# Softmax rows turned by DMA through DRAM, in 16-bit halves, instead of on TensorE: two attention and two expert layers on one core

## The chip, the cores and the metric

The kernel runs on one core of one Trainium2 chip. The metric is the device time of one execution in microseconds; lower is better. The kernel before takes 2253.72 us, the median of 3 runs (2252.45 to 2257.0).

## What is computed

Eight sequences of 512 tokens, 256 features wide, in float32, go through four layers, each added to its input:

```python
x = x + attn_a(layernorm(x))      # 16 heads of 64, a distance penalty per head
x = x + experts(layernorm(x))     # RMS norm, best 2 of 8 experts, gated MLP
x = x + attn_b(layernorm(x))      # 8 heads of 128, rotary embedding
x = x + experts(layernorm(x))

# both attentions, per head
s = q @ k.T                       # plus penalty, or scaled; causal mask
p = softmax(s, axis=-1)           # [512 queries, 512 keys]
out = (p @ v) @ w_out
```

Only the causal half of `s` is computed: for each tile of 128 queries, numbered `it`, the keys up to its own tile. That makes 4 row blocks of 128, 256, 384 and 512 columns, 1280 columns in all, ten 128x128 squares per head.

## The kernel before, in words

**Order of the work.** `layer` (L1133) walks through 64 steps, one for each sequence `b` (8) and group `g` (8). A group is 128 feature columns: two heads in attention a, one in attention b. `Attention.step` (L503) writes out TensorE's order by hand (L120 keeps it so); the tile framework orders the other engines and the queues, and puts in the waits. A step has: the scores of the current group (`scores`, L356, in three banks); the transposes of the group before (`turn`, L436); the projection of queries and keys of the next group (`project`, L327); pieces of other work (`extra`), such as values, output projection, norms, the expert layer's routing; and last the average of the group before (`average`, L461). So a group's scores open one step and its average closes the next.

**One group.** `scores` multiplies queries with keys into PSUM; DVE adds the penalty or mask and takes the row minimum of the negated scores (L407); ACT takes the exponential and the row sum (L417). After the third bank DVE inverts the sums (L428), and the rows are divided in place in the tile `S` (L434): the 512-column block on DVE, the other three on POOL. `turn` then transposes the ten squares of a head on TensorE into PSUM (L449), in three banks, and ACT (L459), for one bank of the second head DVE (L457), copies them to `PT`. `average` takes `PT` as the moving operand, with the values as weights (L476), four matmuls per head of 512, 384, 256 and 128 columns.

**Buffers.** `S` has four buffers, `PT` two, `qk` (queries and keys of a group in one tile) two, `tmp` three. PSUM has eight banks, all under one tag.

**Expert layers.** `Experts` sorts tokens by expert during the attention layer (`sorting`, L917) and then runs 71 blocks of 128 rows (`run`, L1049): POOL gathers rows (L939), TensorE transposes and multiplies, POOL scatters. `flush` (L1192) says at which block the pieces left over from attention are run, the last transposes (L1185) and the last average among them.

**SP's queue** issues the loads, the stores of normed rows (`h_all`, L619) and of the residual (`x_mid`, L621), and the loads of expert results (L1078), in order.

Of the kernel before, what the change touches and what calls it, by code (L numbers as in the profile page):

```python
# [36 lines left out]
F32 = mybir.dt.float32  # L38
BF16 = mybir.dt.bfloat16
I32 = mybir.dt.int32  # L40
AF = mybir.ActivationFunctionType
ALU = mybir.AluOpType
# [19 lines left out]
S_OFF = {3: 0, 2: 512, 0: 896, 1: 1024}  # L62
S_BANKS = [(3,), (2, 0), (1,)]

P_OFF = {0: 0, 1: 512, 3: 896, 2: 1024}
P_BANKS = [(0,), (1, 3), (2,)]
PACKED = 1280
# [18 lines left out]
AHEAD = 3  # L86
# [7 lines left out]
def layers(  # L94
# [109 lines left out]
    step_p = iota([P, TOTAL], [[P, TOTAL]], "step_p")  # L204
    spare = iota([P, TOTAL], [[P, TOTAL]], "spare", 1, 4 * PLANE)
    tiles = iota([P, 2, NB * NT], [[32, 2], [1, NB * NT]], "tiles", 0, 64)
    before = const.tile([P, P], F32, tag="before", name="before")
    nc.vector.tensor_scalar(before, lane, part, None, ALU.is_gt)
    ones = const.tile([P, P], F32, tag="ones", name="ones")
    nc.vector.memset(ones, 1.0)  # L210

# [68 lines left out]
    class Attention:  # L280
# [46 lines left out]
        def project(self, b, g, j):  # L327
# [3 lines left out]
            if j == 0:  # L331
                self.qk[b, g] = work.tile([P, 2, T], F32, tag="qk", name=f"qk_{key}")
            qk = self.qk[b, g]
# [10 lines left out]
            if kind == "b":  # L344
                h = DB // 2
                rot = work.tile([P, T], F32, tag="tmp", bufs=3, name=f"rot_{key}_{j}")
                nc.vector.tensor_tensor(rot[0:h], pp[h:P], sin_sb[h:P], ALU.mult)
                nc.vector.tensor_tensor(rot[h:P], pp[0:h], sin_sb[0:h], ALU.mult)
                nc.vector.tensor_tensor(qk[:, j, :], pp, cos_sb, ALU.mult)  # L349
                nc.gpsimd.tensor_tensor(qk[:, j, :], qk[:, j, :], rot, ALU.add)  # L350
            elif j == 0:
                nc.scalar.mul(qk[:, 0, :], pp, DA**-0.5)
            else:
                nc.vector.tensor_copy(qk[:, 1, :], pp)  # L354

        def scores(self, b, g, n):  # L356
# [3 lines left out]
            qk = self.qk[b, g]  # L360
            if n == 0:
                rows = []
                for i in range(nh):
                    rows.append(
                        (
                            work.tile([P, PACKED], F32, tag="S", bufs=4, name=f"S_{key}_{i}"),
# [5 lines left out]
                if kind == "a":  # L372
                    add = []
                    for i in range(nh):
                        a = work.tile([P, T], F32, tag="tmp", bufs=3, name=f"ali_{key}_{i}")
# [14 lines left out]
            at = {it: S_OFF[it] - S_OFF[bank[0]] for it in bank}  # L390
            for it in bank:
                w = (it + 1) * P
                for i in range(nh):
# [3 lines left out]
                        lhsT=qk[r, 0, it * P : (it + 1) * P],  # L397
                        rhs=qk[r, 1, 0:w],
# [3 lines left out]
            for i, (S, nm, sums) in enumerate(self.S[b, g]):  # L402
                for it in bank:
                    w = (it + 1) * P
                    s = S[:, S_OFF[it] : S_OFF[it] + w]
# [19 lines left out]
            if n == len(S_BANKS) - 1:  # L425
                del self.qk[b, g], self.add[b, g]
                for S, nm, sums in self.S[b, g]:
                    nc.vector.reciprocal(sums, sums)  # L428
                    for it in (3, 2, 0, 1):
                        s = S[:, S_OFF[it] : S_OFF[it] + (it + 1) * P]  # L430

                        mine = it == 3 or (b, g) == (NB - 1, NQ - 1)
                        eng = nc.vector if mine else nc.gpsimd
                        eng.tensor_scalar(s, s, sums[:, it : it + 1], 1.0, ALU.mult, ALU.mult)  # L434

        def turn(self, b, g, i, n):  # L436

            key = f"{self.kind}_{b}_{g}_{i}"
            S = self.S[b, g][i][0]
            if n == 0:  # L440
                self.PT[b, g, i] = work.tile([P, PACKED], F32, tag="PT", name=f"PT_{key}")
            bank = P_BANKS[n]
            base = P_OFF[bank[0]]
            tp = ps.tile([P, T], F32, tag="ps", bufs=8, name=f"tp_{key}_{n}")
            width = 0
            for jt in bank:
                for it in range(jt, NT):
                    o = P_OFF[jt] - base + (it - jt) * P
                    nc.tensor.transpose(  # L449
                        tp[:, o : o + P],  # L450
                        S[:, S_OFF[it] + jt * P : S_OFF[it] + (jt + 1) * P],
                        ident,
                    )
                    width += P
            pt = self.PT[b, g, i][:, base : base + width]
            if n == 0 and i == 1:
                nc.vector.tensor_copy(pt, tp[:, 0:width])  # L457
            else:
                nc.scalar.copy(pt, tp[:, 0:width])  # L459

        def average(self, b, g):  # L461
            kind, nh = self.kind, self.nh
            key = f"{kind}_{b}_{g}"
            del self.S[b, g]
# [8 lines left out]
            for jt in range(NT):  # L473
                for i in range(nh):
                    c0 = (g % 2) * P + i * cols
                    nc.tensor.matmul(  # L476
                        op[i * cols : (i + 1) * cols, jt * P : T],
                        lhsT=v[:, jt, c0 : c0 + cols],
                        rhs=PT[i][:, P_OFF[jt] : P_OFF[jt] + T - jt * P],
                        start=(jt == 0),  # L480
                        stop=(jt == NT - 1),
# [21 lines left out]
        def step(self, last, cur, after, extra):  # L503
# [3 lines left out]
            def scores(n):  # L507
                if cur:
                    self.scores(*cur, n)

            def turn(i, *banks):
                if last:
                    for n in banks:
                        self.turn(*last, i, n)

            def project(j):
                if after and after not in there:
                    self.project(*after, j)

            if self.kind == "a":  # L520
# [818 lines left out]
```

## Time and profile before

| | before |
|---|---|
| median of 3 runs | 2253.72 us |
| the profiled execution | 2251.17 us |
| its span | 2249.4 us |
| attention a, about | 16 to 936 us |
| experts, first layer | 936 to 1177 us |
| attention b | 1177 to 1995 us |
| experts, second layer | 1995 to 2249 us |
| granted TensorE clock, mean | 0.994 |
| HBM read, written | 67.02 MB, 39.60 MB |

All times below are microseconds from the start of the span. In lines of the order of time the columns are start, length, engine, source line, operation, the tile written and the tiles read, and how many instructions were merged; in brackets stands how long the engine had been idle and what released it. Lines of the chain that ended last have start, length, engine, tile, line and count. A float32 matmul appears as two instructions, one for each pass. SPq is SP's queue of DMA issues: the length there is that of issuing, not of the transfer.

### The profile page before, as it was taken

What the parts mean: (1) busy time and instruction counts of PE and PEld (TensorE: products, weight loads), DVE (VectorE), ACT (ScalarE), POOL (GpSimd) and SP (SyncE); (2) the same over time, 40 slices, a digit from 0 to 9 for tenths busy, and PEclk for the clock granted to TensorE, in tenths of its full rate; (3) what the DMA queues carried; (4) which work ended last, traced back from release to release, by engine and by line L of the source; (5) the groups of instructions that cost most, each with busy time, mean ns of one, the idle gap of its engine ahead of it and who ended that gap; (6) DMA issues with size and microseconds to landing.
All of it is one profiled execution on the core that took longest, in us unless ns stands there. A gap on an engine that the chain in (4) does not pass through costs nothing.

```text
span 2249.4 us, 33585 instructions
## 1 busy us (share of the span) xinstructions
PE 2191.5 (97%) x10513; PEld 1430.1 (64%) x10513; DVE 1585.7 (70%) x4817; ACT 961.6 (43%) x2784; POOL 967.7 (43%) x1337
## 2 busy tenths in 40 slices
PE   8999999999999999999999999999999999999995
PEld 5666666666666666656656666666666666666663
DVE  4566666666666687687687676777767678868768
ACT  4555555555555545323334334334433433332331
POOL 5443434343424343366654344333434343346662
PEclk9999999999999999999999999999999999999998
DMA  7100000000000000232220010110101000042237
GB/s 247 38 20 10 18 12 8 22 4 26 1 29 1 29 6 29 103 107 84 86 81 21 10 38 15 34 33 15 47 6 43 8 31 1 19 139 78 85 97 254
DMA packets 78382, 108.80 MB, mean 48 GB/s; under 512 B 9568, under 2 KB 64000, under 8 KB 78208
## 3 DMA queue, kind: packets, MB, share of 16 engines
q1 hardware_dynamic: 62656, 67.58, 9.2%
q0 software_dynamic: 13632, 37.24, 5.2%
q8 instruction: 87, 1.43, 0.3%
q10 hardware_dynamic: 1920, 1.84, 0.2%
q14 instruction: 87, 0.71, 0.1%
HBM read 67.02 MB, written 39.60 MB: 47 GB/s over the span
## 4 chain that ended last, share of the span: by engine, by line
PE 88%; DVE 7%; DMA 1%; issue 1%; ACT 1%; POOL 1%; SPq 0%; DVEq 0%; another core or an unknown queue 0%; ACTq 0%
PE hp_f L982 10%; PE pp_b L337 9%; PE pp_a L337 9%; PE op_a L476 6%; PE sp_a L395 6%; PE tp_a L449 6%; PE sp_b L395 6%; PE op_b L476 5%; PE yp_a L494 5%; PE yp_b L494 5%; PE y_f L1021 5%; PE vp_a L318 4%; PE vp_b L318 4%; PE tp_b L449 3%; PE gtp_f L953 1%
## 5 line engine op out<-in xcount | busy, mean ns | idle before, releaser
L417 ACT ACTIVATE S_a<-S_a,nm_a 128x512 f32<-128x512 f32 (+3 forms) x512 | 280.1, 548 | 311.4 <-DVE nm_a L407 311.2
L350 POOL TENSOR_TENSOR qk_b<-qk_b,rot_b 128x512 f32<-128x512 f32 x128 | 163.1, 1274 | 457.0 <-DVE qk_b L349 434.0
L376 POOL TENSOR_SCALAR ali_a<-alibi 128x512 f32<-128x512 f32 x128 | 79.4, 620 | 454.3 <-DVE nm_a L407 442.0
L982 PE MATMUL hp_f<-we,hT_f 128*128 x544 | 257.8, 596 | 7.6 <-issue 3.9
L417 ACT ACTIVATE S_b<-S_b,nm_b 128x512 f32<-128x512 f32 (+3 forms) x256 | 142.8, 558 | 236.6 <-DVE nm_b L407 228.6
L407 DVE CUSTOM_DVE_ANT_0 S_a<-sp_a,ali_a 128x512 f32<-128x512 f32 (+3 forms) x512 | 215.9, 487 | 30.7 <-PE sp_a L395 28.5
L434 POOL TENSOR_SCALAR S_a<-S_a,sum_a 128x384 f32<-128x384 f32 x378 | 203.1, 554 | 34.6 <-DVE sum_a L428 24.3
L1033 POOL DMA_INDIRECT y_f<-y_f,row_f x142 | 143.5, 1010 | 117.5 <-DVE y_f L1032 58.6
L407 DVE CUSTOM_DVE_ANT_0 S_b<-sp_b,mask 128x512 f32<-128x512 f32 (+3 forms) x256 | 119.3, 484 | 89.1 <-PE sp_b L395 88.9
L395 PE MATMUL sp_b<-qk_b 128*128 128x512 f32 (+3 forms) x512 | 170.5, 436 | 5.5 <-POOL qk_b L350 5.5
L939 POOL DMA_INDIRECT g_f<-h_all_f,token_f x142 | 144.1, 1015 | 61.9 <-issue 39.6
L449 PE MATMUL tp_a<-ident,S_a 128*128 128x128 f32 x1280 | 166.0, 276 | 4.0 <-DVE O_a L484 3.3
L994 ACT ACTIVATE u_f<-u_f 128x256 f32<-128x256 f32 x142 | 59.2, 417 | 256.2 <-DVE u_f L993 176.5
L449 PEld LDWEIGHTS tp_a<-ident,S_a 128*128 128x128 f32 x1280 | 141.3, 142 | 35.1 <-issue 21.6
L476 PE MATMUL op_a<-PT_a,V_a 128*64 128x384 f32 (+3 forms) x1024 | 156.3, 442 | 4.8 <-DVE PT_a L457 2.6
L1021 PEld LDWEIGHTS y_f<-we,aT_f 128*128 128x128 f32 x568 | 108.3, 192 | 77.4 <-issue 58.2
L395 PE MATMUL sp_a<-qk_a 64*128 64x512 f32 (+3 forms) x1024 | 155.5, 443 | 0.9 <-DVE qk_a L354 0.9
L459 ACT COPY PT_a<-tp_a 128x512 f32<-128x512 f32 (+1 forms) x320 | 139.1, 496 | 29.1 <-PE tp_a L449 27.3
L1021 PE MATMUL y_f<-we,aT_f 128*128 x568 | 147.4, 383 | 4.0 <-ACT aT_f L1012 4.0
L476 PE MATMUL op_b<-PT_b,V_b 128*128 128x512 f32 (+3 forms) x512 | 148.6, 433 | 0.0
L993 DVE TENSOR_TENSOR u_f<-hp_f,be 128x512 f32<-128x512 f32 x142 | 98.1, 691 | 65.3 <-PE hp_f L982 27.5
L982 PEld LDWEIGHTS hp_f<-we,hT_f 128*128 128x128 f32 x544 | 92.7, 190 | 76.5 <-issue 70.5
(205 smaller groups left out, 4455.2 us busy)
## 6 DMA issues: line engine op xcount, KB each, us to landing
h_all_f<-hn_f SPq DMA_DIRECT2D x64, 128.0 KB
xm_f<-x_mid_f SPq DMA_DIRECT2D x16, 512.0 KB
yg_f<-y_f SPq DMA_DIRECT2D x32, 256.0 KB
yg_f<-y_f SPq DMA_DIRECT2D x56, 128.0 KB
we<-w_dram SPq DMA_DIRECT2D x8, 512.0 KB
x_mid_f<-x SPq DMA_DIRECT2D x8, 512.0 KB
x_mid_f<-xm_f SPq DMA_DIRECT2D x8, 512.0 KB
x<-x_in_dram SPq DMA_DIRECT2D x7, 512.0 KB
```

The costliest lines, as they stand in the source:

```text
L318: nc.tensor.matmul(vp[:, k, :], lhsT=self.xT[b][:, c, t * P : (t + 1) * P], rhs=wv[:, c, q * 2 * P : (q + 1) * 2 * P], start=(c == 0), sto ...
L337: nc.tensor.matmul(pp, lhsT=w[:, c, g * P : (g + 1) * P], rhs=self.xT[b][:, c, :], start=(c == 0), stop=(c == NC - 1),)
L350: nc.gpsimd.tensor_tensor(qk[:, j, :], qk[:, j, :], rot, ALU.add)
L395: nc.tensor.matmul(sp[i][:, at[it] : at[it] + w], lhsT=qk[r, 0, it * P : (it + 1) * P], rhs=qk[r, 1, 0:w], start=True, stop=True,)
L407: nc.vector.tensor_tensor_reduce(out=s, in0=sp[i][:, at[it] : at[it] + w], in1=add[i][:, T - w : T], scale=scale, scalar=float(np.finfo(np ...
L417: nc.scalar.activation(s, s, AF.Exp, bias=nm[:, it : it + 1], scale=-1.0, accum_out=sums[:, it : it + 1],)
L434: eng.tensor_scalar(s, s, sums[:, it : it + 1], 1.0, ALU.mult, ALU.mult)
L449: nc.tensor.transpose(tp[:, o : o + P], S[:, S_OFF[it] + jt * P : S_OFF[it] + (jt + 1) * P], ident,)
L476: nc.tensor.matmul(op[i * cols : (i + 1) * cols, jt * P : T], lhsT=v[:, jt, c0 : c0 + cols], rhs=PT[i][:, P_OFF[jt] : P_OFF[jt] + T - jt * P],
L494: nc.tensor.matmul(yp[:, 0:D], lhsT=o[:, c, t * P : (t + 1) * P], rhs=wo[:, half * HALF + c, :], start=(c == 0), stop=(c == HALF - 1),)
L982: nc.tensor.matmul(hp, lhsT=h[:, c * P : (c + 1) * P], rhs=we_sb[:, bass.DynSlice(wat + c * 2 * FI, 2 * FI)], start=(c == 0), stop=(c == N ...
L1021: nc.tensor.matmul(yp, lhsT=aT[:, c * P : (c + 1) * P], rhs=we_sb[:, bass.DynSlice(wat + NC * 2 * FI + c * D, D)], start=(c == 0), stop=(c ...
```

## The change

`turn` and its place in the step are gone. `scores` now ends with a call of `send`, which divides the rows and, for each head, splits each 32-bit number into its two 16-bit halves in a tile `apart`: on ACT, but for head 1 in attention a the second half on POOL. SP stores `apart` in a DRAM tile `away`; then SP issues, for each head, one transposing load of 16-bit elements from `away` into `PT`, which lays the two halves of each number side by side again. For head 1 in attention a all four blocks are divided on DVE. `average` walks the new layout with six matmuls per head, of 256 or 128 columns, with a strided moving operand.

Queries and keys each get a tile of their own, in a ring of three. `S` has three buffers, `tmp` two. In the expert layers the gathered rows take buffers of `apart`, activations those of `qk` or `PT`; some index constants become bf16; the counting matmuls (L718) are bf16. The loads of expert results in attention b go to `S` instead of `tmp`. The last average and what follows it run at later blocks of the expert layer (the new `turns`).

```diff
-S_OFF = {3: 0, 2: 512, 0: 896, 1: 1024}
+S_AT = {0: 0, 2: 1, 1: 4, 3: 6}
 S_BANKS = [(3,), (2, 0), (1,)]
-P_OFF = {0: 0, 1: 512, 3: 896, 2: 1024}
-P_BANKS = [(0,), (1, 3), (2,)]
-PACKED = 1280
+BLOCKS_ROW = 10
+PACKED = BLOCKS_ROW * P
+AVERAGE = [((0, 1), 0), ((1,), 1), ((2, 3), 0), ((2, 3), 1), ((2, 3), 2), ((3,), 3)]
...
-AHEAD = 3
+AHEAD = 7
...
-            if j == 0:
-                self.qk[b, g] = work.tile([P, 2, T], F32, tag="qk", name=f"qk_{key}")
-            qk = self.qk[b, g]
+            qk = work.tile([P, T], F32, tag="qk", bufs=3, name=f"qk_{key}_{j}")
+            self.qk[b, g, j] = qk
...
-                            work.tile([P, PACKED], F32, tag="S", bufs=4, name=f"S_{key}_{i}"),
+                            work.tile([P, PACKED], F32, tag="S", bufs=3, name=f"S_{key}_{i}"),
...
+                self.send(b, g)
+
+        def send(self, b, g):
+            kind, nh = self.kind, self.nh
+            last = (b, g) == (NB - 1, NQ - 1)
+            sent = []
+            for i, (S, nm, sums) in enumerate(self.S.pop((b, g))):
+                key = f"{kind}_{b}_{g}_{i}"
+                nc.vector.reciprocal(sums, sums)
+                for it in (3, 2, 0, 1):
+                    s = S[:, S_AT[it] * P : (S_AT[it] + it + 1) * P]
+                    eng = nc.vector if it == 3 or i == 1 or last else nc.gpsimd
+                    eng.tensor_scalar(s, s, sums[:, it : it + 1], 1.0, ALU.mult, ALU.mult)
+                halves = S.bitcast(U16).rearrange("p (w s) -> p s w", s=2)
+                apart = work.tile([P, 2, PACKED], U16, tag="apart", name=f"apart_{key}")
+                nc.scalar.copy(apart[:, 0, :], halves[:, 0, :])
+                if i == 1 and not last:
+                    nc.gpsimd.tensor_copy(apart[:, 1, :], halves[:, 1, :])
+                else:
+                    nc.scalar.copy(apart[:, 1, :], halves[:, 1, :])
+                away = dram.tile([P, 2, PACKED], U16, tag="away", bufs=4, name=f"away_{key}")
+                nc.sync.dma_start(out=away, in_=apart)
+                sent.append(away)
+            for i, away in enumerate(sent):
+                PT = work.tile([P, PACKED], F32, tag="PT", name=f"PT_{kind}_{b}_{g}_{i}")
+                nc.sync.dma_start_transpose(
+                    out=PT.bitcast(U16).rearrange("p (n w) -> p n w", n=BLOCKS_ROW),
+                    in_=away.rearrange("p s w -> (p s) w"),
+                )
+                self.PT[b, g, i] = PT
...
-            for jt in range(NT):
+            for its, jt in AVERAGE:
+                n = len(its)
+                first = S_AT[its[0]] + jt
+                step = S_AT[its[-1]] - S_AT[its[0]] if n > 1 else 1
                 for i in range(nh):
                     c0 = (g % 2) * P + i * cols
+                    rows = PT[i].rearrange("p (n w) -> p n w", n=BLOCKS_ROW)
                     nc.tensor.matmul(
-                        op[i * cols : (i + 1) * cols, jt * P : T],
+                        op[i * cols : (i + 1) * cols, its[0] * P : (its[-1] + 1) * P].rearrange(
+                            "p (n w) -> p n w", n=n
+                        ),
                         lhsT=v[:, jt, c0 : c0 + cols],
-                        rhs=PT[i][:, P_OFF[jt] : P_OFF[jt] + T - jt * P],
+                        rhs=rows[:, first : first + step * (n - 1) + 1 : step, :],
                         start=(jt == 0),
-                        stop=(jt == NT - 1),
+                        stop=(jt == its[-1]),
                     )
...
+            self.scores(*cur, 0)
             if self.kind == "a":
-                scores(0)
-                scores(1)
-                scores(2)
-                turn(0, 0, 1, 2)
+                self.scores(*cur, 1)
+                self.scores(*cur, 2)
                 project(0)
                 extra(1)
-                turn(1, 0, 1, 2)
                 project(1)
                 extra(2)
             else:
-                scores(0)
                 project(0)
-                turn(0, 0)
-                scores(1)
+                self.scores(*cur, 1)
+                self.scores(*cur, 2)
                 project(1)
-                turn(0, 1, 2)
-                scores(2)
                 extra(1)
                 extra(2)
...
-        turns = (0, 2, 2, 2, 3, 5, 8, 10, 12, 14)
+        turns = (6, 6, 6, 7, 9, 12, 14, 16, 18)
...
-        for n, piece in zip((16, 18, 20, 22, 25, 28), exp.sorting(1), strict=True):
+        for n, piece in zip((20, 22, 24, 26, 29, 32), exp.sorting(1), strict=True):
```

## The prediction

> **What bounds the kernel now.** I read the page first for the busiest engine, then the chain that ended last for what that engine does, then the pieces of that chain step by step, and last the order of time on the other engines and on SP's queue.
>
> ```profile
> PE 2191.5 (97%) x10513; PEld 1430.1 (64%) x10513; DVE 1585.7 (70%) x4817; ACT 961.6 (43%) x2784; POOL 967.7 (43%) x1337
> ...
> PE 88%; DVE 7%; DMA 1%; issue 1%; ACT 1%; POOL 1%; SPq 0%; DVEq 0%; another core or an unknown queue 0%; ACTq 0%
> ```
>
> TensorE is the bound: 97% busy and 88% of the chain. The other engines have a third of their time or more to spare, and DMA carries almost nothing in the attention stages. In the stretch from 566.36 to 680.78 us, one sequence of attention a, the busy times are PE 114.38 of 114.42 us, DVE 72.57, ACT 61.26, POOL 43.45, DMA share 0.05. So work taken from TensorE is worth its full time there, until something else is late. The pieces of the chain show one step (L503) after another; each begins with the scores:
>
> ```profile
> 568.66 2.36 PE sp_a L395 x16
> ...
> 579.10 2.36 PE sp_a L395 x16
> ...
> 592.99 2.36 PE sp_a L395 x16
> ...
> 610.33 2.36 PE sp_a L395 x16
> ...
> 624.22 2.36 PE sp_a L395 x16
> ...
> 635.86 2.36 PE sp_a L395 x16
> ...
> 650.48 2.36 PE sp_a L395 x16
> ...
> 667.93 2.36 PE sp_a L395 x16
> ```
>
> The next sequence begins at 683.09. The steps are 10.44, 13.89, 17.34, 13.89, 11.64, 14.62, 17.45 and 15.16 us long, 114.4 together: 14.3 on average, but unequal. The same view gives attention b, from 1345.92 to 1448.43: 14.03, 9.20, 12.57, 15.75, 12.30, 9.72, 13.08, 15.86 us, 102.5 together.
>
> **What is removed.** The chain shows ten tp_a transposes as a piece of 1.24 us, 124 ns each, two pieces per step of a; in b the ten of one head take 1.24 us a step. 64 x 2.48 + 64 x 1.24 = 238 us of TensorE time go. (The page's 166.0 + 90.8 us for L449 count overlapping ends.) With them go ACT's evictions, per step of a 3 x 576 + 2 x 376 ns = 2.5 us, and 0.68 us of DVE's.
>
> **What is added, beside other work.** The averages have the same columns in 6 matmuls per head instead of 4. In the trace the time of sp, op and yp matmuls follows the columns alone (op_b: 1280 columns, two passes, 2.16 us; sp_b, with other shapes, 2.16 us), so this is 0; at most 16 more weight loads of 137 ns that outlast 107 ns of streaming, 0.25 us a step of a if 8 of them show. I take 0. ACT gets the copies of the halves, 1280 elements from SBUF: its exponentials go from 386 ns (128 columns) to 715 (512), 0.86 ns a column, so about 1.25 us a copy; three a step of a, 3.75 us, less the 2.5 removed: 61 + 10 = 71 us per sequence of a. DVE gets three divisions more per step of a (0.42 + 0.3 + 0.2 us), less 0.68. POOL gives those three back (1.66 us) for one copy of 1280 elements, 1.6 us by L376's 620 ns for 512, 3.2 us by L350's 1274; both end before ACT's copies. All stay under 75 us where TensorE's rest is 94.6: no engine becomes the bound by its busy time. The bf16 counting matmuls, the changed buffers of the expert stages, AHEAD 7 and the shifted flush I take at 0 +- 5 us: the last average waits behind six expert blocks that have their own work, and the second sorting ends at block 32 where its first gather is at 37, 5 x 3 us of cover. The ring of three 512-column tiles for queries and keys lets the third tile free as soon as the scores have read it: 0. S has three buffers for four; the tile needed next is free after head 0's copies, about S+10.4 (S is the start of a step's scores), and is next written at S+11.8+1.2: 0, but with 2.5 us of cover only.
>
> **What is added, on the path.** The transposed rows must be there for the average, which closes the *next* step; TensorE is in order, so everything from the next scores on stands behind that wait. So the time from S to the scores two steps later can't fall below the length of this chain, L. Its start is in the trace (S = 579.10):
>
> ```profile
> 584.92 0.49 ACT L417 ACTIVATE S_a<-S_a,nm_a 128x256 f32<-128x256 f32 x1
> 585.04 0.18 DVE L428 RECIPROCAL sum_a<-sum_a 128x4 f32<-128x4 f32 x1 [1.37 <-ACT S_a L417]
> ...
> 585.39 1.77 POOL L434 TENSOR_SCALAR S_a<-S_a,sum_a 128x384 f32<-128x384 f32 x3 [0.58 <-DVE sum_a L428]
> ```
>
> Exponentials end at S+6.3, POOL has divided head 0 at S+8.0. Two copies on ACT: S+10.5; head 1's: S+11.8. Each head is then stored, 655,360 bytes. The nearest row is SP's store of 512 KB, on which the load after it waits:
>
> ```profile
> 164.47 0.37 SPq L621 DMA_DIRECT2D x_mid_f<-x  x1
> 167.44 0.38 SPq L134 DMA_DIRECT2D x<-x_in_dram  x1
> ...
> 278.90 0.37 SPq L621 DMA_DIRECT2D x_mid_f<-x  x1
> 283.37 0.38 SPq L134 DMA_DIRECT2D x<-x_in_dram  x1
> ```
>
> 3.0 and 4.5 us, so 4.1 for the larger one: head 0 is in DRAM at S+14.7, head 1 at about S+16. SP waits that long before it issues the transposing loads. Behind it on SP stand h_all and x_mid stores (read only by the experts), the next x (tens of us early) and, in b, the y rows of the next sequence (used a step later): 4 to 8 us late, none on the path.
>
> No row shows a transposing load. Call X its transport, with 1.5 us fixed (3.0 to 4.5 less the 1.8 to 2.1 us that 512 KB need at the 247 GB/s of the first slice or somewhat more). The Trainium skill has two prices. *VectorE: DVE Perf Modes* (The three transpose paths, and its rules) speaks against the change: 1309 ns by DMA for one 128x128 two-byte block where TensorE takes 390, with the rule to transpose on TensorE where PSUM will do. A head has 20 such blocks, X = 26.2 us. *DMA: Bandwidth & Descriptors* (Latency and other measured facts) has 261 GB/s for a large one: X = 2.5. Its 350 to 400 GB/s for contiguous data would be X about 1.8, a gain that I keep as the lower end. I take 2.5: the first price is of a single small block, fixed part included, while the nearest row, the 512 KB store, shows plain transfers at the second's order of size.
>
> Two transposing loads in a row: S+14.7+1.5+2X = S+21.2; the average, 2.3 us, ends at S+23.5; 0.5 for queues: L(a) = 19 + 2X = 24. For b the trace has the last exponential at 9.1 us after the scores' start and POOL done at 11.2; without the transposes scores 1 and 2 come some 1.2 us sooner and DVE has less between them, so 9.0; two copies, 11.5; stored, 15.6; one load, 19.6; average, 21.8; with 0.7 for order, L(b) = 20 + X = 22.5.
>
> Now the steps: 2.48 or 1.24 us off each, and any two together no shorter than L. Rolled on, a sequence of a takes 102.6 us (12.1 + 14.9 + 15.0 + 12.7 of long steps and two pairs stretched to 24), not the 94.6 of TensorE alone; one of b 98.8, not 92.6. Saved: 8 x 11.8 + 8 x 3.7 = 94 + 30 us, not 238. Eight go back at the start, where step 0's rows queue behind the weights that fill DMA to about 35 us (its average is at 33.88 now). The profiled execution took 2251.2 us, span 2249.4 with 1.8 around it, 2.5 below the median of 2253.7. 2251.2 - 124 + 8 = 2135; beside the median, 2138. I say **2140**.
>
> **Rivals.** *The transposing load is slow, and its wait replaces the transposes.* Place: the average at L476. Price in the same roll-on: X = 4 gives 2207, 4.5 gives 2242, 5 gives 2282, 6 gives 2362, 7 gives 2447. It decides from X = 4.6 us (about 140 GB/s). For it: nothing in the trace transposes, and two heads pay it in series per step of a; four transfers of 0.66 MB in 12.8 us are 205 GB/s, close to the 247 of the busiest slice. Against: the 261 GB/s. Its middle is 2360; at 1309 ns a block it would be 4290. *All is hidden.* Shorter stores and X = 1.8, or the copies sooner: L(a) under 20, and TensorE bounds again: 2251 - 238 + 8 = 2020. For it: 25 us per two steps are two thirds idle for every other engine; against: the short pairs of 19.4 and 20.6 us need a chain that no store of 3 us leaves. *In-order engines hold the copies.* If ACT's copies stand behind value evictions and the next scores' exponentials, or SP's transposing loads behind stores that wait for normed rows, L grows by 3 to 5 us: 2200 to 2260, no change.
>
> **How the numbers follow.** Likeliest, the partly hidden chain, 2080 to 2200: 0.37. Hidden almost whole, below 2080: 0.15. Held back, 2200 to 2249: 0.03; within 0.2% (2249 to 2258, about what a measurement can tell): 0.03. Slow load, 2258 to 2500: 0.31; very slow, above: 0.11. So faster 0.55, same 0.03, slower 0.42. The range from 2040 to 2500 leaves out about 0.06 below and 0.11 above; the likeliest case's own is 2080 to 2200.
>
> **What would show it.** Right: no L449 rows; PE busy down some 240 us; idle PE before op_a, released by the loads of PT, about 60 us in a and 50 in b; pairs of short steps near 24 us, long steps at their own length; copies of about 1.25 us on ACT; stores landing in about 4 us and the transposing loads in about 4 and 6.5. Wrong: loads landing after 6 us or more, steps of a all of one length (L/2); or S and PT buffers, ACT or SP named as what scores wait for.

## The result and the profile after

The changed kernel takes 2286.9 us (median of 4 runs, 2285.1 to 2295.5) where the kernel before takes 2254.0 beside it: ratio 1.015, interval 1.012 to 1.018. It is slower; I had forecast 2140. The profiled execution has a span of 2283.0 us, 33.6 more than before.

The page's busy times, and the first entry of its table of DMA queues (packets, MB, share of 16 engines):

```profile
PE 2064.2 (90%) x9329; PEld 1332.0 (58%) x9329; DVE 1615.2 (71%) x4943; ACT 1120.8 (49%) x2593; POOL 958.8 (42%) x1211
...
q1 hardware_dynamic: 587968, 319.28, 51.6%
```

TensorE's busy time fell by 127 us, not by 238, and it now idles some 219 us where it idled 58. No other engine is a bound by its busy time. The view of waits says what it idles for (us in all, times, longest):

```profile
PE op_a L484 <- DMA PT_a<-away_a: 79.0, 43, 12.4
...
PE op_b L484 <- DMA PT_b<-away_b: 45.6, 18, 8.9
...
PE sp_b L401 <- POOL qk_b L356: 17.3, 11, 3.4
```

The averages wait for their transposed rows, as the chain L of the prediction has it (L: from the start S of a step's scores to the scores two steps later). The third line was not in it: in b scores also wait for queries and keys, which GpSimd finishes.

By stages, from the first scores of a to its last: attention a 897.8 us (902.1 before), from its last scores to the first scores of b 276.5 (260.4), attention b 812.5 (801.2), from its last scores to the end 279.8 (269.6). So a gains 4, b loses 11, and the two passages between attention and experts lose 16 and 10. A sequence from the second to the sixth takes 112.2 us in a (114.4 before) and 102.3 in b (102.5), where I count from the second scores of b; the first sequence of a takes 122.5 (105.2), the first nine steps of b 112.1 (100.5).

Where nothing disturbs it, the chain is as long as I said. The timeline of one step of a whose scores start at S = 563.66, from SP and from TensorE (start, duration, idle time ahead in brackets):

```profile
574.38 1.54 SPq L456 DMA_DIRECT2D away_a<-apart_a  x2
...
578.13 5.62 SPq L460 DMA_TRANSPOSE PT_a<-away_a  x2
...
584.03 0.65 PE L484 MATMUL op_a<-PT_a,V_a 128*64 128x256 f32 x2
...
585.97 2.38 PE L484 MATMUL op_a<-PT_a,V_a 128*64 128x256 f32 x22 [1.29 <-DMA PT_a<-away_a]
...
588.27 1.13 PE L401 MATMUL sp_a<-qk_a,qk_a 64*128 64x512 f32 x4
```

Stores at S+10.7, transposing loads from S+14.5, the second head's rows at S+22.3, the scores after next at S+24.6; the prediction had 24. In b the undisturbed chain is 22.4 us, where it had 22.5. Its parts differ from mine in both directions: an undisturbed store lands in 2.9 to 3.5 us (4.1), one transposing load about 5 us after SP begins to issue it (4.0), two of them about 8 (6.5). In the step above, two stretches of 3.0 us show what the DMA engines do behind the second line (stretch, length, busy time of TensorE, its weight loads, VectorE, ScalarE and GpSimd with counts, granted clock, share of the DMA engines, GB/s):

```profile
579.25:582.25 3.00, 3.00 (x17) 1.51 (x14) 2.94 (x13) 2.21 (x7) 0.00 (x0) 1.00 1.05 217
582.25:585.25 3.00, 2.42 (x7) 0.73 (x5) 1.55 (x8) 2.75 (x11) 2.15 (x4) 1.00 1.08 218
```

The DMA engines are fully busy throughout, 3.0 us for each load. So X is about 3 us and the fixed part about 2. SP itself is held by each transposing load for 3.0 us in a and 2.8 in b (medians; the shortest 2.5), where a store holds it 0.34.

But not all steps are undisturbed. SP's queue three steps earlier in the same sequence:

```profile
515.13 2.04 SPq L616 DMA_DIRECT2D h_all_f<-hn_f  x2
517.22 1.26 SPq L456 DMA_DIRECT2D away_a<-apart_a  x2
520.71 6.81 SPq L460 DMA_TRANSPOSE PT_a<-away_a  x2
527.58 1.04 SPq L616 DMA_DIRECT2D h_all_f<-hn_f  x2
528.72 0.40 SPq L618 DMA_DIRECT2D x_mid_f<-x  x1
531.74 0.38 SPq L139 DMA_DIRECT2D x<-x_in_dram  x1
532.18 0.97 SPq L456 DMA_DIRECT2D away_a<-apart_a  x2
537.55 6.39 SPq L460 DMA_TRANSPOSE PT_a<-away_a  x2
```

The load of x (L139) waits 3.0 us for the landing of x_mid, and the row stores stand behind it: they are issued at S+13.8 (S = 518.41), not S+10.7. They also land later, in 5.3 to 6.3 us beside the load of x, and the transposing loads start at S+19.1. L is 29.9 us here, and 27.3 in the step before it.

### The profile page after: what moved, and what is told of

The parts are those of the page before. It is cut to its first block, busy times and chain, and to the rows that moved or that the text cites. A ratio compares the mean times of both kernels' runs of the same rounds, so it can differ in the third digit from the quotient of the medians.

```text
span 2283.0 us, 31747 instructions
## 1 busy us (share of the span) xinstructions
PE 2064.2 (90%) x9329; PEld 1332.0 (58%) x9329; DVE 1615.2 (71%) x4943; ACT 1120.8 (49%) x2593; POOL 958.8 (42%) x1211
## 3 DMA queue, kind: packets, MB, share of 16 engines
q8 instruction: 77, 1.26, 0.2%
## 4 chain that ended last, share of the span: by engine, by line
PE 44%; DVE 8%; DMA 4%; POOL 1%; issue 1%; SPq 1%; ACT 0%; DVEq 0%; another core or an unknown queue 0%; POOLq 0%; ACTq 0%
PE hp_f L980 9%; PE pp_b L343 8%; PE op_b L484 6%; PE sp_b L401 5%; PE yp_b L504 5%; PE y_f L1029 4%; PE vp_b L325 3%; DMA PT_b<-away_b 2%; PE gtp_f L951 1%; PE atp_f L1015 1%; DVE rot_b L354 1%; DVE rot_b L353 1%; DVE S_b L413 1%; DVE qk_b L355 1%; DVE u_f L1001 1%
## 5 line engine op out<-in xcount | busy, mean ns | idle before, releaser
L484 PE MATMUL op_a<-PT_a,V_a 128*64 128x256 f32 (+1 forms) x1536 | 197.0, 385 | 82.7 <-DMA PT_a<-away_a 79.0
L980 PE MATMUL hp_f<-we,hT_f 128*128 x512 | 246.3, 604 | 7.2 <-DVE u_f L1001 5.8
L413 DVE CUSTOM_DVE_ANT_0 S_a<-sp_a,ali_a 128x512 f32<-128x512 f32 (+3 forms) x512 | 216.7, 487 | 29.9 <-PE sp_a L401 26.8
L484 PEld LDWEIGHTS op_a<-PT_a,V_a 128*64 128x64 f32 x1536 | 122.1, 151 | 169.0 <-DMA PT_a<-away_a 63.8
L484 PE MATMUL op_b<-PT_b,V_b 128*128 128x256 f32 (+1 forms) x768 | 166.5, 371 | 45.6 <-DMA PT_b<-away_b 45.6
L450 ACT COPY apart_a<-S_a 128x1280 uint16<-128x1280 uint16 x128 | 161.0, 1258 | 83.6 <-POOL S_a L447 81.1
L484 PEld LDWEIGHTS op_b<-PT_b,V_b 128*128 128x128 f32 x768 | 144.9, 206 | 74.6 <-issue 40.0
L401 PE MATMUL sp_b<-qk_b,qk_b 128*128 128x512 f32 (+3 forms) x512 | 162.1, 440 | 17.3 <-POOL qk_b L356 17.3
L494 DVE COPY O_a<-op_a 128x512 f32<-128x512 f32 x64 | 44.1, 689 | 172.7 <-PE op_a L484 172.6
L401 PE MATMUL sp_a<-qk_a,qk_a 64*128 64x512 f32 (+3 forms) x1024 | 157.8, 447 | 7.0 <-DVE qk_a L360 6.8
L447 DVE TENSOR_SCALAR S_a<-S_a,sum_a 128x512 f32<-128x512 f32 (+3 forms) x323 | 141.5, 487 | 4.1
```

The source lines that it names most:

```text
L401: nc.tensor.matmul(sp[i][:, at[it] : at[it] + w], lhsT=q[r, it * P : (it + 1) * P], rhs=k[r, 0:w], start=True, stop=True,)
L413: nc.vector.tensor_tensor_reduce(out=s, in0=sp[i][:, at[it] : at[it] + w], in1=add[i][:, T - w : T], scale=scale, scalar=float(np.finfo(np ...
L450: nc.scalar.copy(apart[:, 0, :], halves[:, 0, :])
L484: nc.tensor.matmul(op[i * cols : (i + 1) * cols, its[0] * P : (its[-1] + 1) * P].rearrange("p (n w) -> p n w", n=n), lhsT=v[:, jt, c0 : c0 ...
L980: nc.tensor.matmul(hp, lhsT=h[:, c * P : (c + 1) * P], rhs=we_sb[:, bass.DynSlice(wat + c * 2 * FI, 2 * FI)], start=(c == 0), stop=(c == N ...
```

## Experiments

They ran on several chips. Beside them the kernel before took 2255.2 us (e1 to e4), 2232.8 (e5 to e8, and again 2232.9 for e13 to e15) and 2246.8 (e9 to e12). With attention untouched (before, and e5 on another chip) a sequence agrees to 0.1 us; what differs is the expert stages (260.4 and 249.0 us for the first). So I compare ratios to the kernel before and mean lengths of the second to sixth sequences:

| kernel | ratio to before (interval) | a, us | b, us |
|---|---|---|---|
| before | 1 | 114.4 | 102.5 |
| changed | 1.015 (1.012 to 1.018) | 112.2 | 102.3 |
| e1 rows not awaited | 0.975 (0.973 to 0.977) | 100.6 | 101.0 |
| e2 average a step later | 1.018 (1.016 to 1.021) | 109.3 | 107.6 |
| e3 row stores issued by ACT | 1.020 (1.018 to 1.022) | 112.3 | 104.0 |
| e4 side edits alone | 1.007 (1.005 to 1.008) | 115.1 | 102.7 |
| e5 before, late flush | 1.000 (0.999 to 1.001) | 114.4 | 102.5 |
| e6 early flush | 1.017 (1.016 to 1.019) | 112.9 | 102.5 |
| e7 x load later | 1.006 (1.005 to 1.008) | 109.1 | 102.3 |
| e8 filler | 1.032 (1.030 to 1.033) | 112.1 | 106.2 |
| e9 one head by DMA | 0.996 (0.995 to 0.997) | 107.9 | 102.8 |
| e10 e1, keys' addition on DVE | 0.951 (0.949 to 0.952) | 100.6 | 96.0 |
| e11 e7, last but one average later | 1.007 (1.005 to 1.008) | 109.2 | 102.1 |
| e12 e9, b on TensorE | 1.017 (1.016 to 1.019) | 107.9 | 110.5 |
| e13 keys' addition on DVE | 1.018 (1.017 to 1.020) | 112.4 | 104.2 |
| e14 e9, e7 and e13 | 0.993 (0.992 to 0.995) | 107.9 | 103.0 |
| e15 changed again | 1.017 (1.015 to 1.018) | 112.9 | 102.5 |

My theory at the start: the wait for the rows is the whole loss. The rival: other work of the change is.

**e1.** The averages read the query weights, so the result leaves the transposed rows out; they are still made, stored and loaded.

```diff
-                    rows = PT[i].rearrange("p (n w) -> p n w", n=BLOCKS_ROW)
+                    rows = wq.rearrange("p c n -> p (c n)")[:, 0:PACKED].rearrange("p (n w) -> p n w", n=BLOCKS_ROW)
```

> The averages take a constant tile (query weights) in place of the turned rows; stores and transposing loads still run, nobody reads what they bring. Leaves out the softmax rows in the average. Theory, the wait for the turned rows (and the slower TensorE after it) is the loss: attention falls to TensorE's own 94.6 us a sequence in a and 92.6 in b, so about 2250 - 238 + 20 for edges that remain = 2020 to 2060. Rival, the DMA traffic or the fuller ACT, POOL and SP slow the other engines, whoever waits for rows: above 2200.

It fell between the two, at 2195.7 us. Without any wait for rows the kernel is 59.5 us faster than before, where my forecast with its row wait had 116: the row wait can't be the whole loss. In a it is worth 11.6 us a sequence; the 100.6 left are still above TensorE's work, since it waits 2.8 us in each sequence for VectorE's keys and norms. In b the rows' wait is worth 1.3, and the profile of e1 shows what took its place (waits, then the timeline of GpSimd and TensorE about one start of scores):

```profile
PE sp_b L401 <- POOL qk_b L356: 49.0, 18, 3.5
```

```profile
1458.87 1.73 POOL L447 TENSOR_SCALAR S_b<-S_b,sum_b 128x384 f32<-128x384 f32 x3 [1.41 <-DVE sum_b L443]
1460.57 1.26 POOL L356 TENSOR_TENSOR qk_b<-qk_b,rot_b 128x512 f32<-128x512 f32 x1
...
1461.89 1.12 PE L401 MATMUL sp_b<-qk_b,qk_b 128*128 128x512 f32 x2 [2.72 <-POOL qk_b L356]
```

GpSimd divides S for 1.7 us and only then adds the rotation to the keys of the next step; the scores stand behind both. A second floor lies under the first.

**e2.** The average moves from the end of the next step into the middle of the one after, and the rows' loads are issued a step later in a.

```diff
                 self.scores(*cur, 2)
                 project(0)
+                if first:
+                    self.average(*first)
+                if last:
+                    self.fetch(*last)
+                self.send(*cur)
```

> Each average is moved some 4 to 6 us later, into the middle of the step after next, the transposing loads of a behind it; nothing else is cheaper. Theory, the chain from scores to average is about 4 us longer than the two steps that cover it: about 97 us a sequence in a and 94 in b, 2090 to 2140, faster than both kernels. Rival, throughput of SP and DMA (two loads of 2.9 us that hold SP, four transfers a step) is the limit: no better than 2250.

The rows' wait shrank (op_a for PT_a 15.4 us in all, where the changed kernel has 79.0), and other waits grew in its place:

```profile
PE sp_b L402 <- POOL qk_b L357: 77.9, 35, 5.8
...
PE sp_a L402 <- DVE qk_a L361: 43.0, 26, 3.8
```

With the average ahead of the second projection, queries and keys come too late. a gains 3 us a sequence, b loses 5. The time is the rival's, but keys and not throughput are the reason.

**e3.** The row stores go through ACT's queue in place of SP's.

```diff
-                nc.sync.dma_start(out=away, in_=apart)
+                nc.scalar.dma_start(out=away, in_=apart)
```

> The stores of the halves are issued on ACT's queue, so they no longer stand on SP behind the stores of normed rows and behind the next x load, which waits some 3 us for its buffer's store. Theory, order on SP adds 3 to 5 us to two chains of each sequence of a: 10 to 35 us faster than the changed kernel, 2250 to 2277. Rival, the transfers compete in the DMA engines whatever the queue: within 5 us of 2287.

No gain: 2301, with op_a's wait at 101 us. ScalarE issues the stores of step 3 on time, at S+10.9, but SP's order changed as well. SP's queue in a sequence whose step 2 starts at S = 394.76:

```profile
403.67 4.20 SPq L616 DMA_DIRECT2D h_all_f<-hn_f  x4
408.06 1.10 SPq L618 DMA_DIRECT2D x_mid_f<-x  x1
409.32 7.55 SPq L460 DMA_TRANSPOSE PT_a<-away_a  x2
```

All of h_all and x_mid now stand ahead of the transposing loads of step 2, whose rows come at S+24.2 where the changed kernel has 22.7. Step 3 grows from 14.5 to 17.4 us, and step 4 falls from 15.7 to 12.7: what one chain gains, the one before it loses.

**e4.** The kernel before, with its transposes on TensorE, and the change's side edits: rows packed by S_AT and averages in six products, bf16 constants, AHEAD 7, late flush.

> The kernel before with the side edits only: six matmuls per average on the new layout, bf16 constants and counting, gathered tiles in place for seven blocks, the later flush; transposes stay on TensorE. Theory, these cost nothing: 2245 to 2262. Rival, six short matmuls per average or the later flush cost: 2265 to 2290, most of the loss.

16 us are lost by the medians, 21 by the profiles, of which that of the kernel before is from another chip: 0.7 us a sequence in a for the six products (a bound of 0.25 us a step was in the prediction; it is 0.09), 0.2 in b, and 17 us in the two expert stages. I put these on the late flush.

**e5.** The kernel before with `AHEAD = 7` and the change's flush, no more.

```diff
-        turns = (0, 2, 2, 2, 3, 5, 8, 10, 12, 14)
+        turns = (0, 6, 6, 6, 7, 9, 12, 14, 16, 18)
```

> The kernel before, with its attention untouched and TensorE's transposes kept; only the pieces that are finished beside the expert blocks come later (project_out, norms and gates at blocks 6 to 18 instead of 2 to 14, the second sorting at 20 to 32 instead of 16 to 28, the next weights at 8 instead of 6) and AHEAD is 7. Theory (the late flush is what e4 lost): the whole +16 us of e4, 2265 to 2273, with the attention stages of before (114.4 and 102.5 us a sequence) and both expert stages longer by 7 to 10 us. Rival (e4's loss came from its six-matmul averages and bf16 constants): no change, 2250 to 2259.

No change, to 0.1%. The late flush costs nothing, as predicted, and my reading of e4 was wrong.

**e6.** The changed kernel with the flush of before, but its first four pieces at block 5.

```diff
-        turns = (6, 6, 6, 7, 9, 12, 14, 16, 18)
+        turns = (5, 5, 5, 5, 6, 8, 10, 12, 14)
```

> The changed kernel, with these pieces back where the kernel before has them, but for the first four, which stay at block 5 because the last rows must come through DRAM first. Theory (late flush, additive): 12 to 17 us under the changed kernel, 2270 to 2276. Rival (the rows of the last step set the start of the pieces, so earlier places only make TensorE wait there): no gain or a loss, 2285 to 2300, with an idle time before op_a or op_b in the first blocks.

No gain (e15, the changed kernel on this chip, has the same ratio), which agrees with e5. What e4 lost in the expert stages stays open: it can be the bf16 constants, or that chip; e4 was not run on another.

**e7.** The next x is loaded two steps later, pinned in SP's order.

```diff
-    more += [((b, 1, 1), lambda b=b: fetch_a(b + 1)) for b in range(NB - 1)]
+    more += [((b, 3, 1), lambda b=b: fetch_a(b + 1)) for b in range(NB - 1)]
```

> The changed kernel, with the load of the next x in attention a issued on SP behind the transposing loads of step 3 instead of straight behind the store of x_mid, so that it no longer holds SP for 3 us in front of step 2's own stores. Theory (what stands on SP is on the path): the pair of steps that took 28.5 to 30 us falls to 26 to 27, 2 to 3 us in each of 7 sequences: 2265 to 2275. Rival (my prediction's 'none on the path'): no change, 2283 to 2291.

0.9 to 1.1% less than the changed kernel (ratio 1.006 against 1.015 and 1.017), and a at 109.1 us. SP's queue in e7 about the same step of another sequence, whose scores start at S = 399.19:

```profile
408.43 0.40 SPq L618 DMA_DIRECT2D x_mid_f<-x  x1
410.13 1.54 SPq L456 DMA_DIRECT2D away_a<-apart_a  x2
414.94 6.44 SPq L460 DMA_TRANSPOSE PT_a<-away_a  x2
421.42 0.57 SPq L1209 DMA_DIRECT2D x<-x_in_dram  x1
```

The row stores are issued at S+10.9 and the transposing loads at S+15.8; L is 26.8 us, and in the same step of the changed kernel (S = 407.11) 29.7, with stores at S+13.4 and loads at S+19.1. One instruction of 0.4 us, waiting 3 us ahead of the row stores, cost 3.8 us a sequence (e15, on the same chip, has 112.9), 24 us in all. But e7 is still slower than the kernel before: this alone does not turn the sign.

**e8.** Useless products ahead of averages that wait.

```diff
+            for _ in range({("a", 2): 16, ("a", 3): 16, ("b", 1): 28}.get((kind, g), 0)):
+                nc.tensor.matmul(op[:, 0:P], lhsT=ident, rhs=ident, start=True, stop=True)
```

> The changed kernel, with 16 (a, averages of steps 2 and 3) or 28 (b, step 1) useless products of the identity put on TensorE in front of the average that waits for its rows; they are overwritten by the average. Theory (the wait costs twice, once as idle time and again because TensorE then runs at half speed): op_a x22 at 4.0 us and op_b at 4.1 us fall to 2.4, the granted clock rises from 0.964 to 0.98 or more, and 20 to 35 us come back: 2252 to 2267. Rival (the half speed lies in slack, or the products only lengthen the wait): 2280 to 2300.

It missed its aim. In b I put them a step too early, ahead of an average that had no wait, where they only cost their 6.3 us. In a, 16 take 3.7 us, not the 1.7 I had counted. In step 3 the average then ran at full speed, and the step takes 12.9 us where e15, on the same chip, has 13.9 on average; in step 4, where the wait for the first head was shorter than the filler, it takes 17.3 for 16.8. The granted clock rose from 0.964 to 0.977 and the kernel got slower. So in step 3 filling the wait did remove the half speed behind it. Both steps together gain 0.8 us a sequence; what the half speed costs in all, this run doesn't measure.

**e9.** In a, head 1 goes back to TensorE (ten transposes behind the next scores); head 0 goes through DRAM. b as in the changed kernel.

```diff
+                if i == 1:
+                    self.kept[b, g] = S
+                    continue
                 halves = S.bitcast(U16).rearrange("p (w s) -> p s w", s=2)
...
                 self.scores(*cur, 2)
+                if last:
+                    for n in range(3):
+                        self.turn(*last, 1, n)
+                self.send(*cur)
                 project(0)
```

> The changed kernel, but in attention a only head 0's rows go through DRAM; head 1's are transposed on TensorE behind the next scores, as before the change. Attention b as in the changed kernel. Theory (in a the chain from scores to rows is what costs; with one head the second store, the second hold of SP and the 1.25 us copies of head 1 leave it, so that it falls under two steps): L about 19 to 20 us, so a sequence of a is bound by TensorE's own work, 96.9 + 9.1 = 106 us, against 112 in the changed kernel and 114.4 before: 45 us under the changed kernel, ratio to the kernel before 0.99 to 1.0. Rival (queries and keys, or the half-speed clock, set the steps of a): 109 to 112 us a sequence, ratio 1.00 to 1.015.

107.9 us a sequence, every one alike, and the kernel is 0.4% faster than before. The wait for rows in a is gone but for the first step and the last:

```profile
PE op_a L510 <- DMA PT_a<-away_a: 19.0, 2, 9.6
```

Half the transposes by DMA are worth more than all of them, because the chain then fits under two steps. 107.9 is 105.6 us of TensorE's work, near the 97 of its rest and 9.1 of transposes, and 2.3 us of waits of scores for the queries.

**e10.** e1, and in b the keys' rotation is added by VectorE (the result again leaves the rows out).

```diff
-                nc.gpsimd.tensor_tensor(qk, qk, rot, ALU.add)
+                (nc.vector if j else nc.gpsimd).tensor_tensor(qk, qk, rot, ALU.add)
```

> e1 (averages read the query weights in place of the transposed rows, which are left out of the result) with one more edit: in attention b the last addition of the keys' rotation is done by VectorE instead of GpSimd. Theory (in b a second floor stands under the row wait: the keys of the next step wait on GpSimd behind its divisions of S): the waits of sp_b for qk_b of 49 us vanish, b falls from 100.5 us a sequence to 94 to 97, all in all 30 to 45 us under e1. Rival (VectorE's own queue is the floor, GpSimd only its last link): 99 to 102 us a sequence, no change against e1 (ratio 0.97 to 0.98).

b falls to 96.0: with neither floor it comes within 2 us of what TensorE needs (94). The steps of 10.55 us fall to 9.3.

**e11.** e7, with the average of the last step but one at expert block 3.

```diff
             if last and after:
                 self.average(*last)
...
+        return [lambda: att.average(*steps[-2]), lambda: att.average(*last)] + left
```

> The changed kernel with e7's later x load, and with the average of the last step but one of each attention taken out of the attention loop and put at expert block 3, since in the last step of a it waits 12.4 us and of b 8.9 us for its rows with nothing else on TensorE. Theory (this wait is the loss at the entry of both expert stages): 12 and 8 us less than e7, ratio 0.995 to 1.0 where e7 had 1.006, first hp block 10 us after the last scores instead of 21. Rival (the expert blocks then wait for the same rows or for their own tokens): ratio 1.003 to 1.008.

The first block starts at 14.9 us behind the last scores and not at 21.4 (e7, on another chip), but the sixth at 50.2 (47.9 in e7): the time came back as waits for the gathered tokens, 22.9 us where the changed kernel has 2.4.

```profile
PE gtp_f L951 <- DMA g_f<-h_all_f,token_f: 22.9, 7, 8.4
```

So the entry to the experts isn't held by that one wait alone. e1 says the same: no average waits there, and the first passage takes 278.5 us, with 12.2 of waits for tokens. In the changed kernel GpSimd's first gathers wait 18.7 us for the last row store, since they fill the tiles (`apart`) that it reads. That this is the rest was not tried.

**e12.** e9, with b's transposes back on TensorE too; its ring of three single tiles, and with it the second projection behind the last scores, stay.

> As e9 (head 0 of a through DRAM, head 1 on TensorE), and attention b's transposes wholly back on TensorE, with queries and keys still in the ring of three. Theory (b gains nothing by DMA and loses 10 us at the end): a as e9; b 102 to 104 us a sequence; the stage behind b back to before's length: ratio 0.98 to 0.99. Rival (the ring of three, which makes the keys wait until the last scores have read their tile, is what holds b): b 105 us or more a sequence, waits of sp_b for qk_b, ratio 0.995 to 1.01.

b takes 110.5 us where e4, with the same products and transposes, takes 102.7. The profile names it:

```profile
PE sp_b L402 <- POOL qk_b L357: 42.4, 18, 3.1
```

So the ring of three, with the order that it forces, costs b some 7.8 us a sequence: keys may only be projected when the last scores have let go of a tile, and so their rotation ends when the next scores already wait. 4.9 us of it are these waits, the rest is slower work of TensorE, mostly in the projections. A ring of four was not tried, and `S` and `tmp` had one buffer less here than in e4, which no wait names.

**e13.** The changed kernel with e10's edit alone, rows awaited.

> The changed kernel with one edit: in attention b the last addition of the keys' rotation is done by VectorE, not behind GpSimd's divisions of S. Theory (the keys are the floor of b's short steps even where rows are awaited): the steps of 10.55 us fall to 9.3, b from 102.3 us a sequence to 97 to 100, 20 to 35 us under e15, level with the kernel before (ratio 0.998 to 1.006). Rival (the rows set b's pairs of steps, so what a short step gains the wait before the next average takes back): 101 to 103 us a sequence, no more than 8 us under e15, with the idle time before op_b up by as much.

The rival was right in kind, though b came out above its 101 to 103. The waits for keys vanish and the short steps fall to 9.4, but the rows don't come sooner:

```profile
PE op_b L484 <- DMA PT_b<-away_b: 70.8, 25, 9.6
```

47.3 us in the changed kernel on the same chip. The two floors of b lie at one height, and taking one away alone brings nothing.

**e14.** e9, e7 and e13 together.

> e9 (head 1 of a back on TensorE) with the keys' addition on VectorE in b and the later x load. Theory (the remedies add): a at 107.9 us a sequence, b as e13, ratio 0.975 to 0.988, the fastest of all right kernels. Rival (rows set b): ratio 0.993 to 0.998 as e9.

2216.9 us against 2232.9: 0.7% faster than before, the fastest kernel that computes everything, though not as far as the theory of sums had it: b stays at 103.0, since its rows set it (op_b waits 69.3 us).

**e15.** The changed kernel on that chip.

> The changed kernel as it is, on the chip of e13 and e14. All theories: ratio 1.010 to 1.020, a about 112 and b about 102.3 us a sequence, whatever the expert stages take on this chip.

As expected. With e5 as the kernel before on the same chip, its 39.9 us are: a's first sequence +20, the rest of a -13.5, the first passage +15.5, b +9.3, the last passage +8.2, start +0.4.

## Why the prediction was wrong

Sum of the miss, in the profiled executions: forecast -124 + 8 = -116, found +33.6, so 150 us. a's steps and start 82 of them, b 41, the passages 26.

- **Removed.** 238 us was too much. By the start-to-start times of what surrounds them the transposes took 18.2 us a sequence of a and 8.75 of b: 216. With the six products' 0.09 us a step, TensorE alone needs 96.9 and 94.0 us and not 94.6 and 92.6.
- **Other engines.** Right: copies take 1.26 us (the rate that I took it from gives 1.37); VectorE, the busiest, has 75.8 us in a sequence of a. That the other engines are two thirds idle was wrong, VectorE had 72.57 of 114.42 us before. The DMA engines had no such sum: they are busy for 0.77 of the third sequence's 113.2 us, by an estimate 87 us, not a floor yet under TensorE's 97 but the next one.
- **The chain.** Right in length, 24.6 and 22.4 us for 24 and 22.5, and the choice between the two prices of the Trainium skill was right. 655,360 bytes in 3.0 us are 218 GB/s, of the order of the 261 that *DMA: Bandwidth & Descriptors* (Latency and other measured facts) gives from one kernel, without a size; by the 1309 ns a block of *VectorE: DVE Perf Modes* (The three transpose paths) it would have been 26 us. The rival of a slow load, which gives the nearest time (4.6 us decides), is therefore not what happened: the load was fast and the kernel slow, and the nearness is chance. (The busiest slice of the page before has 254 GB/s, its last; the 247 that the prediction calls so is the first. Nothing hangs on it.)
- **The step that failed: "none on the path".** I asked how late SP's neighbours get behind the transposing loads, and not how late the row stores get behind the neighbours. In step 3 of each sequence of a (from step 0) h_all, x_mid and the x load stand ahead of them, and steps 3 and 4 take 28.6 to 31.7 us together where my roll-on has 24.7 (12.6 and 12.1); e7, which removes the x load alone, gets 3 to 4 us of it back, 24 us of the miss of 150. In b the transposing load of the step with h_all and x_mid starts about 1 us later than in the others. My third rival, in-order queues that hold the rows, named the place, with 3 to 5 us, but I gave it 0.03.
- **The second zero: the ring of three, "0".** By e12 it costs b some 7.8 us a sequence when the transposes are back on TensorE; by e1 and e10 the late keys are the floor at 101 us under the row wait, and go when GpSimd no longer adds their rotation behind its divisions. That the ring makes them late is read from e12 and from the order of the code. It is why b, where the transposes' 8.75 us are gone, gained 0.2. I had followed when the third tile comes free, and not what is queued from there: projection, three VectorE operations, GpSimd's divisions, the addition.
- **A wait that costs twice.** Behind such a wait TensorE ran at a lower granted clock, which no term had. In the trace of the changed kernel (two averages, then the granted clock of the same stretches, the third figure from the end):

```profile
1428.75 2.33 PE L484 MATMUL op_b<-PT_b,V_b 128*128 128x256 f32 x12
...
1440.90 4.07 PE L484 MATMUL op_b<-PT_b,V_b 128*128 128x256 f32 x12 [3.34 <-DMA PT_b<-away_b]
```

```profile
1428.75:1431.08 2.33, 2.33 (x14) 2.12 (x13) 2.29 (x5) 1.91 (x2) 1.79 (x2) 1.00 0.01 4
1440.90:1445.00 4.10, 4.10 (x13) 3.50 (x14) 2.40 (x4) 2.42 (x3) 1.51 (x2) 0.59 0.70 197
```

The same work takes 1.74 us longer behind 3.3 us of idle time, at a clock of 0.59. All such averages in the trace together, by an estimate from their lengths, take 24 us longer in a and 16 in b. Of b's one long step (13.8 us, my roll-on 11.4) this is the larger part, and of the 26.3 to 27.3 us that steps 2 and 3 of a take in place of 24 it is 1.6. The Trainium skill (*TensorE: Matmul & The Clock Gate*, Part 1) has half the clock after an idle window of about 3.4 us; here 2.0 and 1.7 us with 0.6 of work between were enough too (op_a 3.97 us for 2.38), while 1.3 to 1.9 us alone mostly were not, and one average of b ran in 2.41 us behind a wait of 3.19.
- **The start and the passages.** +8 was +17 to +20: the first rows' stores are issued at 31.2 us and their transposing loads only at 39.5, behind the weights, and step 1 takes 26.3 us. It is not the rows' wait alone: in e1, which has none, the first sequence still takes 117.0 us, and TensorE waits for biases whose load stands on SP behind the transposing loads of the first steps:

```profile
PE b_ps L225 <- DMA b_p<-b_dram: 14.0, 1, 14.0
```

  The passages, 0 +- 5, lost 16 and 10. The average of the last step but one waits 12.4 and 8.9 us for its rows, as the last step has nothing else for TensorE; my cover ("six expert blocks") was for the last average only. e1 and e11 show that the tokens come next; with that average out of the way the first passage is no shorter.

So no single term carries the miss: the transposes' 216 us were paid out to the row wait in a, to two floors of one height in b, and to the seams.

## What to carry to other kernels

When work leaves the engine that bounds, list everything that it covered, each with its own finish time: several floors may lie within a few us, and the next lowest takes over. For a transfer put on the path, read the issuing queue from the transfer's side, what stands ahead of it and what that waits for, and not only what it delays. And move a part first: half the transposes by DMA kept the chain under the steps and won where all of them lost.

## What was not expected of the hardware

- A transposing load holds SP's queue for about 3 us (medians 3.0 in a, 2.8 in b), a plain store of the same 655,360 bytes for 0.34.
- A granted clock of 0.59 behind a wait of 3.3 us, and 1.6 to 1.8 us for most averages behind waits of 2 to 3 us.
- From chip to chip this kernel's time differs by 1% (2232.8 to 2255.2 us for the kernel before), by the profiles in its expert stages and not in its attention stages.
